# Batch-normalised pair products on one Trainium2 core: the long rows taken in descending instead of ascending order

## The chip, the core and the metric

The kernel runs on one core of one Trainium2 chip. The metric is the device time of one execution in microseconds; the kernel before takes 1881.34 us (median of three runs, 1881.19 to 1881.53). The engines named below are TensorE (PE in the profile), VectorE (DVE), ScalarE (ACT), GpSimd (POOL) and SyncE (SP), which here issues the output transfers. SBUF is the on-chip memory that the engines work in, PSUM the smaller one that TensorE writes to.

## What is computed

Two inputs of 1024 batch rows, 39 fields and 16 elements are multiplied pair by pair, normalised per pair over the batch, and weighted by one 16x16 matrix. There are 741 pairs (r, c) with c < r, and each pair gives a 16x16 block for each batch row: 777 MB of float32 output from about 5 MB of input.

```python
B, F0, F1, E, C = (256, 39, 39, 16, 1)          # the inputs that come have 1024 in place of B
_ROWS, _COLS = np.tril_indices(F1, k=-1)         # 741 pairs
cross = xj[:, rows, :, None] * xi[:, cols, None, :]
mean = jnp.mean(cross, axis=(0, 2, 3), keepdims=True)
var = jnp.mean(jnp.square(cross - mean), axis=(0, 2, 3), keepdims=True)
normed = (cross - mean) * jax.lax.rsqrt(var + BN_EPS)
normed = normed * gamma[None, :, None, None] + beta[None, :, None, None]
out = normed[:, :, None, :, :] * W[None, None, :, :, :]
```

## The kernel before

The kernel first computes a scale s and a shift t for each pair, so that the normalised product is s * (xi * xj) + t. A **row** r holds the pairs (r, 0) to (r, r-1). The 1024 batch rows are 128 partitions by 8 blocks, and a **tile** is one row for two blocks (T = 2): 2 x r slices of 256 elements per partition.

The output buffer `y_sb` is two **slots** of 76 slices. The middle row 19 comes first, as four tiles of half a slot each. Then each long row r shares its slot with the short row 38 - r, so that a slot is always full; row 38 has no partner and fills a slot alone.

```python
half = T * (F - 1)                                # 76
mid = (F - 1) // 2                                # 19
tiles = [(mid, t0, t0 // T * half // 2) for t0 in range(0, NT, T)]
slot = 0
for r in range(mid + 1, F):                       # 20, 21, ... 38
    for t0 in range(0, NT, T):
        tiles.append((r, t0, slot * half))
        if r < F - 1:
            tiles.append((F - 1 - r, t0, slot * half + T * r))
        slot ^= 1
```

Each tile goes through four stages. `scale_xi` (line 167, GpSimd) makes xi * s for the row, into one of two buffers. `products` (lines 145 and 147) makes 16 products for each of the two blocks, each over all pairs of the row; ScalarE takes the first ones and GpSimd the last 4 to 6 of each block. Rows of at most 4 pairs are made on VectorE instead (lines 180 and 190).

```python
split = E - (POOL_I_FIRST[n] if n < 3 else POOL_I_LONG if tiles[n][0] > LONG else POOL_I)
for t in range(T):
    for i in range(E):
        product(n, nc.scalar if i < split else nc.gpsimd, t, i, xs[:, t])
```

`finish` adds the shift and multiplies by the weight. VectorE does that for most pairs, one instruction for each pair (line 284). A share of the pairs goes to GpSimd (lines 270 and 273); in rows over 33, eight pairs, whose shift ScalarE adds (line 268) and which GpSimd weights in two steps of four pairs.

```python
if long:                                          # r > 33
    share = POOL_PAIRS_LONG                       # 8
elif RAW < n < 10:
    share = POOL_PAIRS_FIRST                      # 3
else:
    share = int(r * POOL_SHARE + 0.5) if r > SHORT else 0
p0 = p1 - share                                   # p1 is r // 2 in long rows, else r
... # GpSimd's pairs p0 to p1
for t in range(0, T, size):                       # size is 2, but 1 for tile 1
    for c0, c1 in zip(bounds(n), bounds(n)[1:]):
        for c in [*range(c0, min(c1, p0)), *range(max(c0, p1), c1)]:
            stt(...)                              # line 284, VectorE
        store(n, c0, c1, t, t + size)
```

`bounds` cuts a tile into the pieces in which it is stored: `FIRST_PIECES` for the first tiles, then one piece up to row 24 and two above. In rows over 24 the last piece goes out as two stores, one for each block.

```python
FIRST_PIECES = (
    (0, 1, 3, 6, 10, 14, 19), (0, 4, 9, 14, 19), (0, 4, 11, 19), (0, 9, 19), (0, 10, 20), (0, 9, 18), (0, 10, 20), (0, 9, 18)
)
step = 1 if r > ONE and c1 == r else t_to - t_from        # ONE is 24
for t in range(t_from, t_to, step):
    nc.sync.dma_start(...)                                # line 209
```

The scales and shifts reach all partitions by groups of rows. `spread` copies a group with TensorE into a PSUM bank, and `apply` (lines 493 to 500, three or four small operations on VectorE) folds in gamma and beta. A group is given as (first row, row behind the last, bank, the tile behind which it is applied).

```python
ROW_GROUPS = (
    (19, 20, 0, None), (20, 21, 1, None), (15, 19, 1, 2), (21, 25, 2, 4), (1, 15, 2, 8), (25, 32, 3, 16), (32, 39, 4, 24)
)
SHORT_GROUP = 4
...
for group in range(1, len(ROW_GROUPS)):
    spread(group)
s_short = spread_of[SHORT_GROUP][0][:, 0]
apply(1)
products(1)
scale_xi(2)
for n in range(1, len(tiles)):
    if n + 2 < len(tiles):
        scale_xi(n + 2)
    finish(n)
    for group, (_, _, _, tile_of) in enumerate(ROW_GROUPS):
        if n == tile_of:
            apply(group)
    if n + 1 < len(tiles):
        products(n + 1)
    if n == 32:
        nc.scalar.copy(xj_short, xj_sb[:, :, 1 : SHORT + 1, :])
```

The framework sets the waits: an instruction that writes slices of `y_sb` waits until the transfers that still read them have landed.

Of the kernel before, what the change touches and what calls it, by code (L numbers as in the profile page):

```python
# [16 lines left out]

ONE, LONG = 24, 33
FIRST_PIECES = (
    (0, 1, 3, 6, 10, 14, 19), (0, 4, 9, 14, 19), (0, 4, 11, 19), (0, 9, 19), (0, 10, 20), (0, 9, 18), (0, 10, 20), (0, 9, 18)  # L20
)


# [6 lines left out]


ROW_GROUPS = (
    (19, 20, 0, None), (20, 21, 1, None), (15, 19, 1, 2), (21, 25, 2, 4), (1, 15, 2, 8), (25, 32, 3, 16), (32, 39, 4, 24)
)
SHORT_GROUP = 4


@with_exitstack
def tile_pair_outer_batchnorm(
# [17 lines left out]
    NB, F, E = xi.shape  # L57
# [8 lines left out]
    mid = (F - 1) // 2  # L66
    tiles = [(mid, t0, t0 // T * half // 2) for t0 in range(0, NT, T)]
    slot = 0
    for r in range(mid + 1, F):
        for t0 in range(0, NT, T):  # L70
            tiles.append((r, t0, slot * half))
            if r < F - 1:
                tiles.append((F - 1 - r, t0, slot * half + T * r))
            slot ^= 1

    RAW = 1
# [58 lines left out]
    def view(n):  # L135
        r, _, u = tiles[n]
        return y_sb[:, u : u + T * r, :].rearrange("p (t n) e -> p t n e", t=T)
# [23 lines left out]
    def scale_xi(n):  # L161
        r, t0, _ = tiles[n]
        if r <= SHORT:
            return
        n0 = first[r]
        xs = scaled.tile([P, T, r, E], F32, tag="xs", name=f"xs_{r}_{t0}")
        nc.gpsimd.tensor_tensor(  # L167
            xs,
            xi_sb[:, t0 : t0 + T, 0:r, :],
            s_sb[:, :, n0 : n0 + r, :].to_broadcast([P, T, r, E]),  # L170
            ALU.mult,
        )
        xs_of[n] = xs

    def products(n):

        r, t0, _ = tiles[n]
        if r <= SHORT:
            xs = scaled_short.tile([P, T, r, E], F32, tag="xs_short", name=f"xs_{r}_{t0}")
            nc.vector.tensor_tensor(  # L180
                xs,
                xi_sb[:, t0 : t0 + T, 0:r, :],
                s_short[:, first[r] : first[r] + r]
                .unsqueeze(1)
                .unsqueeze(3)
                .to_broadcast([P, T, r, E]),
                ALU.mult,
            )
            for t in range(T):
                nc.vector.tensor_tensor(  # L190
                    view(n)[:, t].rearrange("p n (i j) -> p n i j", j=E),
                    xs[:, t].unsqueeze(2).to_broadcast([P, r, E, E]),
                    xj_short[:, t0 + t, r - 1 : r, :].unsqueeze(3).to_broadcast([P, r, E, E]),
                    ALU.mult,
                )
            return
        xs = xs_of.pop(n)
# [5 lines that stand above are left out]
    def store(n, c0, c1, t_from=0, t_to=T):  # L203
        r, t0, _ = tiles[n]
        n0 = first[r]

        step = 1 if r > ONE and c1 == r else t_to - t_from
        for t in range(t_from, t_to, step):
            nc.sync.dma_start(  # L209
                out_v[:, t0 + t : t0 + t + step, (n0 + c0) * EE : (n0 + c1) * EE],  # L210
                view(n)[:, t : t + step, c0:c1, :].rearrange("p t n e -> p t (n e)"),
            )
# [27 lines left out]
    def bounds(n):  # L240
        if n < len(FIRST_PIECES):
            return FIRST_PIECES[n]
        r = tiles[n][0]
        pieces = 1 + (r > ONE)
        return tuple(q * r // pieces for q in range(pieces + 1))

    def finish(n):


        r = tiles[n][0]  # L250
        n0 = first[r]
        y = view(n)
        long = r > LONG
        p1 = r // 2 if long else r
        if long:
            share = POOL_PAIRS_LONG
        elif RAW < n < 10:
            share = POOL_PAIRS_FIRST
        else:
            share = int(r * POOL_SHARE + 0.5) if r > SHORT else 0  # L260
        p0 = p1 - share
        step = POOL_PAIRS_LONG // 2 if long else r
        for c0 in range(p0, p1, step):
            c1 = min(c0 + step, p1)
            for c in range(c0, c1):
                t_c = t_sb[:, n0 + c : n0 + c + 1]
                if long:
                    nc.scalar.activation(y[:, :, c, :], y[:, :, c, :], AF.Identity, bias=t_c)  # L268
                else:
                    nc.gpsimd.tensor_scalar(  # L270
                        y[:, :, c, :], y[:, :, c, :], t_c, 1.0, ALU.add, ALU.mult
                    )
            nc.gpsimd.tensor_tensor(  # L273
                y[:, :, c0:c1, :],
                y[:, :, c0:c1, :],
                w_sb.unsqueeze(1).to_broadcast([P, T, c1 - c0, EE]),
                ALU.mult,
            )

        size = 1 if n == RAW else T  # L280
        for t in range(0, T, size):
            for c0, c1 in zip(bounds(n), bounds(n)[1:]):
                for c in [*range(c0, min(c1, p0)), *range(max(c0, p1), c1)]:
                    stt(  # L284
                        y[:, t : t + size, c, :],
                        y[:, t : t + size, c, :],
                        t_sb[:, n0 + c : n0 + c + 1],
                        w_dve.to_broadcast([P, size, EE]),
                        ALU.add,
                        ALU.mult,  # L290
                    )
                store(n, c0, c1, t, t + size)

    with tc.manual_schedule():
# [180 lines left out]
        def spread(group):  # L475
            r0, r1, bank, _ = ROW_GROUPS[group]
            n0, n1 = first[r0], first[r1 - 1] + r1 - 1
            at = used[bank]
            used[bank] = at + 2 * (n1 - n0)
            ps = ps_st[bank][:, at : used[bank]].rearrange("p (x n) -> p x n", x=2)  # L480
            for r in range(r0, r1):
                nc.tensor.matmul(  # L482
                    ps[:, :, first[r] - n0 : first[r] - n0 + r],
                    pick[:, r, :],
                    stq[:, :, 0:r],
                    start=True,
                    stop=True,
                )
            spread_of.append((ps, n0, n1))

        def apply(group):
            ps, n0, n1 = spread_of[group]
            nc.vector.tensor_mul(ps[:, 1], ps[:, 1], st_sb[:, 0, n0:n1])
            if group == SHORT_GROUP:

                nc.vector.tensor_mul(ps[:, 0], ps[:, 0], st_sb[:, 0, n0:n1])
                nc.vector.tensor_copy(st_sb[:, 0, n0:n1], ps[:, 0])
            else:
                nc.vector.tensor_mul(st_sb[:, 0, n0:n1], ps[:, 0], st_sb[:, 0, n0:n1])
            nc.vector.tensor_add(st_sb[:, 1, n0:n1], ps[:, 1], st_sb[:, 1, n0:n1])  # L500
# [8 lines left out]
        for group in range(1, len(ROW_GROUPS)):  # L509
            spread(group)  # L510
        s_short = spread_of[SHORT_GROUP][0][:, 0]
        apply(1)
        products(1)
        scale_xi(2)

# [6 lines that stand above are left out]
                    apply(group)  # L522
            if n + 1 < len(tiles):
                products(n + 1)
            if n == 32:
                nc.scalar.copy(xj_short, xj_sb[:, :, 1 : SHORT + 1, :])


# [26 lines left out]
```

## Time and profile before

| What | Before |
|---|---|
| Device time, median of 3 | 1881.34 us |
| Span of the profiled execution | 1880.0 us |
| VectorE busy | 1720.4 us (92%) |
| ScalarE busy | 1642.7 us (87%) |
| GpSimd busy | 1531.7 us (81%) |
| Output queue, share of the 16 DMA engines | 98.3% |
| Bytes written | 776.99 MB |

Three parts of the profile matter here. A table by stretch gives, for each stretch of time, the busy time of each engine with its number of instructions, then the TensorE clock, the mean share of the 16 DMA engines that was busy, and GB/s; a share well under 1 in a short stretch is time in which the output queue had nothing to move. The timeline lists instructions in order of time, neighbours of one kind merged, with the idle time before them and what ended it. The groups by shape give the busy time and the mean duration of one instruction.

Times in these views are microseconds from the start of the span. A line number such as L284 is that of the kernel before; in the changed kernel the same line has a number one higher.

### The profile page before, as it was taken

How to read it: one execution, taken by the hardware profiler on the slowest of the kernel's cores; microseconds unless marked ns; L12 is line 12 of the kernel's file. 1: busy time of each engine (PE TensorE's matmuls, PEld its weight loads, DVE VectorE, ACT ScalarE, POOL GpSimd, SP SyncE). 2: the span in 40 equal slices, each digit the busy share in tenths (PEclk: the TensorE clock that was granted, in tenths of full speed). 3: DMA queues.
4: the chain of work that ended last, by engine and by line, in shares of the span. 5: the costliest groups of instructions: out<-in, count | busy, mean ns of one | idle time of the engine just before them, and what ended most of it. 6: DMA issues, size and time to landing. Idle time of an engine off the chain costs nothing. (4 is left out here: it accounts for less than half of the span.)

```text
span 1880.0 us, 9660 instructions
## 1 busy us (share of the span) xinstructions
PE 25.5 (1%) x130; PEld 23.0 (1%) x130; DVE 1720.4 (92%) x2625; ACT 1642.7 (87%) x3416; POOL 1531.7 (81%) x1746
## 2 busy tenths in 40 slices
PE   4000000000000000000000000000000000000000
PEld 4000000000000000000000000000000000000000
DVE  8999999998989898989898989898999999988885
ACT  7998989898989798989898989898988888888883
POOL 8999888888888788888888878787888777777873
PEclk8555555555555555555555555555555555555555
DMA  5999999999999999999999999999999999999999
GB/s 197 384 424 426 430 427 428 429 425 426 425 427 424 424 424 424 424 426 425 424 423 425 424 426 424 416 424 424 422 420 425 423 424 422 420 422 415 426 415 411
DMA packets 63994, 783.63 MB, mean 417 GB/s; under 512 B 4784, under 2 KB 6448, under 8 KB 17072
## 3 DMA queue, kind: packets, MB, share of 16 engines
q1 hardware_dynamic: 62624, 779.72, 98.3%
q10 hardware_dynamic: 1296, 3.29, 0.5%
q14 instruction: 73, 0.60, 0.1%
q8 instruction: 1, 0.02, 0.0%
HBM read 6.00 MB, written 776.99 MB: 416 GB/s over the span
## 5 line engine op out<-in xcount | busy, mean ns | idle before, releaser
L284 DVE SCALAR_TENSOR_TENSOR y_sb<-y_sb,st_sb,w_dve 128x512 f32<-128x512 f32 (+1 forms) x2511 | 1651.0, 738 | 132.1 <-issue 119.7
L145 ACT ACTIVATE y_sb<-xs,xj_sb 128x288 f32<-128x288 f32 (+20 forms) x3194 | 1510.7, 567 | 192.9 <-DMA out_dram<-y_sb 163.8
L147 POOL TENSOR_SCALAR y_sb<-xs,xj_sb 128x416 f32<-128x416 f32 (+29 forms) x1126 | 604.7, 560 | 41.2 <-DMA out_dram<-y_sb 28.0
L273 POOL TENSOR_TENSOR y_sb<-y_sb,w_sb 128x2048 f32<-128x2048 f32 (+3 forms) x155 | 517.1, 3342 | 104.0 <-ACT y_sb L268 94.4
L167 POOL TENSOR_TENSOR xs<-xi_sb,st_sb 128x640 f32<-128x640 f32 (+33 forms) x135 | 184.0, 1363 | 171.3 <-ACT y_sb L145 165.1
L270 POOL TENSOR_SCALAR y_sb<-y_sb,st_sb 128x512 f32<-128x512 f32 x291 | 196.8, 691 | 0.1
L268 ACT ACTIVATE y_sb<-y_sb,st_sb 128x512 f32<-128x512 f32 x160 | 100.2, 708 | 1.9
L190 DVE TENSOR_TENSOR y_sb<-xs,ps 128x1024 f32<-128x1024 f32 (+3 forms) x32 | 24.8, 818 | 0.6
L482 PE MATMUL ps<-y_sb 39*128 39x38 f32 (+37 forms) x76 | 16.5, 398 | 2.9 <-DVE y_sb L468 2.9
L482 PEld LDWEIGHTS ps<-y_sb 39*128 39x128 f32 x76 | 16.3, 329 | 3.1 <-DVE y_sb L468 3.1
L346 ACT ACTIVATE y_sb<-y_sb 128x1248 f32<-128x1248 f32 x8 | 9.9, 1243 | 2.8 <-POOL y_sb L335 2.8
L351 DVE TENSOR_REDUCE y_sb<-y_sb 128x78 f32<-128x1248 f32 x8 | 11.2, 1445 | 0.4 <-ACT y_sb L346 0.4
L335 POOL TENSOR_TENSOR y_sb<-xi_sb,y_sb 128x1248 f32<-128x1248 f32 x4 | 9.2, 2320 | 2.8 <-ACT y_sb L384 2.8
L145 ACT ACTIVATE y_sb<-xi_sb,xj_sb 128x304 f32<-128x304 f32 x24 | 11.4, 540 | 0.0
L232 DVE TENSOR_TENSOR y_sb<-y_sb,w_dve 128x2048 f32<-128x2048 f32 (+4 forms) x6 | 10.7, 1839 | 0.1
L325 DVE TENSOR_REDUCE y_sb<-xi_sb 128x39 f32<-128x624 f32 (+1 forms) x6 | 6.1, 1012 | 3.8 <-DMA xi_sb<-in_r_xi_dram 3.8
L335 POOL TENSOR_TENSOR y_sb<-xj_sb,y_sb 128x1248 f32<-128x1248 f32 x4 | 9.2, 2322 | 0.0
L225 POOL TENSOR_SCALAR y_sb<-y_sb,st_sb 128x512 f32<-128x512 f32 x8 | 6.4, 813 | 1.9 <-ACT y_sb L145 1.9
L371 PE MATMUL ps<-y_sb 128*39 128x79 f32 x48 | 7.5, 323 | 16.0 <-DVE y_sb L351 15.9
L325 DVE TENSOR_REDUCE y_sb<-xj_sb 128x39 f32<-128x624 f32 (+1 forms) x6 | 6.1, 1013 | 0.6 <-DMA xj_sb<-in_r_xj_dram 0.6
L223 ACT ACTIVATE y_sb<-y_sb,st_sb 128x512 f32<-128x512 f32 x9 | 6.5, 800 | 0.2 <-ACT y_sb L145 0.2
L371 PEld LDWEIGHTS ps<-y_sb 128*39 128x39 f32 x48 | 5.5, 168 | 18.0 <-DVE y_sb L351 10.7
(59 smaller groups left out, 35.2 us busy)
## 6 DMA issues: line engine op xcount, KB each, us to landing
out_dram<-y_sb SPq DMA_DIRECT2D x25, 2304.0 KB, 14.6
out_dram<-y_sb SPq DMA_DIRECT2D x12, 4352.0 KB, 15.4
out_dram<-y_sb SPq DMA_DIRECT2D x12, 4096.0 KB, 16.3
out_dram<-y_sb SPq DMA_DIRECT2D x10, 4608.0 KB, 14.6
out_dram<-y_sb SPq DMA_DIRECT2D x12, 3840.0 KB, 17.5
out_dram<-y_sb SPq DMA_DIRECT2D x21, 2048.0 KB, 17.0
out_dram<-y_sb SPq DMA_DIRECT2D x12, 3584.0 KB, 18.1
out_dram<-y_sb SPq DMA_DIRECT2D x12, 3328.0 KB, 18.1
```

The lines of the kernel that those rows point to most:

```text
L145: nc.scalar.activation(y, src, AF.Copy, scale=scale)
L147: engine.tensor_scalar(y, src, scale, 1.0, ALU.mult, ALU.mult)
L167: nc.gpsimd.tensor_tensor(xs, xi_sb[:, t0 : t0 + T, 0:r, :], s_sb[:, :, n0 : n0 + r, :].to_broadcast([P, T, r, E]), ALU.mult,)
L190: nc.vector.tensor_tensor(view(n)[:, t].rearrange("p n (i j) -> p n i j", j=E), xs[:, t].unsqueeze(2).to_broadcast([P, r, E, E]), xj_short ...
L268: nc.scalar.activation(y[:, :, c, :], y[:, :, c, :], AF.Identity, bias=t_c)
L270: nc.gpsimd.tensor_scalar(y[:, :, c, :], y[:, :, c, :], t_c, 1.0, ALU.add, ALU.mult)
L273: nc.gpsimd.tensor_tensor(y[:, :, c0:c1, :], y[:, :, c0:c1, :], w_sb.unsqueeze(1).to_broadcast([P, T, c1 - c0, EE]), ALU.mult,)
L284: stt(y[:, t : t + size, c, :], y[:, t : t + size, c, :], t_sb[:, n0 + c : n0 + c + 1], w_dve.to_broadcast([P, size, EE]), ALU.add, ALU.mult,)
L325: nc.vector.tensor_reduce(total[:, t0:t1, part(x)], sources[x][:, t0:t1], AX.X, ALU.add)
L335: nc.gpsimd.tensor_tensor(devs[n % 7], sources[x][:, t0 : t0 + T], shift[:, x : x + 1, :].unsqueeze(3).to_broadcast([P, T, F, E]), ALU.sub ...
L371: nc.tensor.matmul(ps_g[acc][0:F, 0 : 2 * F + 1], lhs, fb[:, t], start=t == 0, stop=t == NT - 1)
L482: nc.tensor.matmul(ps[:, :, first[r] - n0 : first[r] - n0 + r], pick[:, r, :], stq[:, :, 0:r], start=True, stop=True,)
```

## The change

The long rows behind the middle row come in descending order, 38 to 20, each still with its short row. The aim is that the kernel ends with small tiles instead of tiles that fill a slot. Four things go with it:

- The row groups are cut differently, ordered as the rows now come up, and applied later: row 38's group follows tile 1, and no group is applied ahead of tile 1.
- Tiles 4 and 5, now of row 38, are stored in four pieces; the entries for tiles 6 and 7 go.
- The share of three pairs for GpSimd holds for tiles 2 and 3 alone. Tiles 4 to 9, which it covered before, are now long tiles or tiles with a rule of their own.
- The copy of the short rows' xj to PSUM follows tile 5 instead of tile 32, since row 1 comes up at tile 9.

```diff
 FIRST_PIECES = (
-    (0, 1, 3, 6, 10, 14, 19), (0, 4, 9, 14, 19), (0, 4, 11, 19), (0, 9, 19), (0, 10, 20), (0, 9, 18), (0, 10, 20), (0, 9, 18)
+    (0, 1, 3, 6, 10, 14, 19), (0, 4, 9, 14, 19), (0, 4, 11, 19), (0, 9, 19), (0, 10, 19, 29, 38), (0, 10, 19, 29, 38)
 )
@@
 ROW_GROUPS = (
-    (19, 20, 0, None), (20, 21, 1, None), (15, 19, 1, 2), (21, 25, 2, 4), (1, 15, 2, 8), (25, 32, 3, 16), (32, 39, 4, 24)
+    (19, 20, 0, None), (38, 39, 1, 1), (34, 38, 1, 4), (1, 5, 1, 5), (29, 34, 2, 28), (5, 10, 2, 29),
+    (25, 29, 3, 68), (10, 14, 3, 69), (20, 25, 4, 100), (14, 19, 4, 101),
 )
-SHORT_GROUP = 4
+SHORT_GROUP = 3
@@
-    for r in range(mid + 1, F):
+    for r in range(F - 1, mid, -1):
@@
-        elif RAW < n < 10:
+        elif RAW < n < 4:
             share = POOL_PAIRS_FIRST
@@
         s_short = spread_of[SHORT_GROUP][0][:, 0]
-        apply(1)
         products(1)
@@
-            if n == 32:
+            if n == 5:
                 nc.scalar.copy(xj_short, xj_sb[:, :, 1 : SHORT + 1, :])
```

## The prediction, made before the changed kernel was run

> **What bounds the kernel now.** I read four views in this order: the page, tables of busy time by stretch, the timeline around the stretches that stood out, and the groups by shape for durations. From the page, the busy share of the 16 DMA engines by slice, and the bytes:
>
> ```profile
> DMA  5999999999999999999999999999999999999999
> ...
> HBM read 6.00 MB, written 776.99 MB: 416 GB/s over the span
> ```
>
> After the first slice the output queue is busy everywhere. So the time is a startup, plus 777 MB at the queue's own rate, plus the gaps in which the queue has nothing to move. The order of the rows changes no byte; it can only move gaps. I looked for them stretch by stretch (the last two columns are DMA share and GB/s):
>
> ```profile
> 64.00:65.00 1.00, 0.00 (x0) 0.00 (x0) 1.00 (x3) 1.00 (x4) 1.00 (x1) 0.50 0.31 123
> 68.00:69.00 1.00, 0.00 (x0) 0.00 (x0) 1.00 (x3) 1.00 (x4) 1.00 (x3) 0.50 0.00 0
> 78.00:80.00 2.00, 0.00 (x0) 0.00 (x0) 2.00 (x5) 2.00 (x5) 2.00 (x4) 0.50 0.81 340
> 300.00:500.00 200.00, 0.00 (x0) 0.00 (x0) 187.80 (x287) 183.11 (x416) 167.20 (x214) 0.50 1.00 427
> 1215.00:1216.00 1.00, 0.00 (x0) 0.00 (x0) 1.00 (x2) 1.00 (x3) 1.00 (x4) 0.50 0.48 196
> 1830.00:1831.00 1.00, 0.00 (x0) 0.00 (x0) 1.00 (x2) 1.00 (x3) 1.00 (x2) 0.50 0.10 39
> ```
>
> The full rate is 427 GB/s. One pair of a tile (two batch blocks, 262,144 bytes) takes 0.614 us of queue, and a tile of row 38 takes 23.3 us. Adding up the shortfalls of the shares, the queue is short by 2.6 us between 64 and 70, 0.4 us at 78 to 80, 0.8 us at 1215 to 1217 (by the bytes written so far, where row 31 gives way to row 32), 0.5 us at 1662 to 1666 and 1.0 us at 1733 to 1738 (rows 36 and 37), and 1.6 us at 1830 to 1834 (row 38). These sum to about 7 us, and not all of it is in an order's reach. The timeline shows why row 38 starves:
>
> ```profile
> 1819.21 19.84 DVE L284 SCALAR_TENSOR_TENSOR y_sb<-y_sb,st_sb,w_dve 128x512 f32<-128x512 f32 x30 [5.04 <-issue]
> 1819.21 5.01 ACT L268 ACTIVATE y_sb<-y_sb,st_sb 128x512 f32<-128x512 f32 x8
> 1821.92 9.00 POOL L273 TENSOR_TENSOR y_sb<-y_sb,w_sb 128x2048 f32<-128x2048 f32 x2 [8.47 <-ACT y_sb L268]
> 1826.79 15.35 ACT L145 ACTIVATE y_sb<-xs,xj_sb 128x608 f32<-128x608 f32 x22 [2.57 <-DMA out_dram<-y_sb]
> 1830.89 7.49 POOL L147 TENSOR_SCALAR y_sb<-xs,xj_sb 128x608 f32<-128x608 f32 x10
> ```
>
> The columns are start, duration, engine, line, operation, shape and count. A row-38 tile fills a whole slot of the two. Its products may start only when the tile two before has left that slot. Every store of its first piece then waits for products (15.35 us on ScalarE), half the biases (2.7 us), and two weightings on GpSimd (9.0 us), which end at 1830.92; 0.3 us later the queue runs again. That is a chain of 27.1 us + 0.3 us. What covers it is the tile between (23.3 us) plus what the older tile still has queued when the products start. Here the queue went dry at 1830.0, 3.2 us after the next products started at 1826.79; that lead exists because the older tile's last piece goes out as two stores, and the second (19 pairs of one block, 5.8 us) is not waited for by the first half of the products. 27.4 - 23.3 - 3.2 = 0.9 us short, of the order of the 1.6 us seen.
>
> **What the Trainium skill says.** *DMA: Bandwidth & Descriptors*, Specifications, gives a fabric ceiling of 435 GB/s and a limit of about 358 GB/s for one core's HBM. The trace agrees with the first as the wall (427) and not with the second. The same page, Anatomy of one DMA, puts most of a transfer's fixed cost of about 2 us (fitted there on another issuing path) into the write receipt before the semaphore. The trace fits: the half tile ended at 1830.0 - 5.8 = 1824.2, and its waiter started 2.6 us later. *Perfetto Trace Analysis*, Optimization Strategy, says that a gap repeating on the saturated engine can mean too few buffers; the row-38 chain is such a case.
>
> **The change, part by part.** I number tiles as in the list: 0 to 3 are the middle row, tile 4 is the first behind it: row 20 before, row 38 after.
>
> *Groups.* One group of three small VectorE operations (46.92 to 47.63) goes from ahead of tile 1 to behind it, and a later group at 71.48 goes. Tile 1 gains 0.7 us, tile 2 nothing, tile 3 about 0.5 us. The 64 to 70 gaps stay, as tile 2's pieces come no earlier; the 0.4 us at 78 to 80 goes. The queue then runs from 69.2 through the rest of tiles 2 and 3: (7 + 8 + 19) x 0.614 = 20.9 us, dry at 90.1.
>
> *Tile 4 becomes row 38.* Durations come from row 38's own groups in the trace before:
>
> ```profile
> L145 ACT ACTIVATE y_sb<-xs,xj_sb 128x608 f32<-128x608 f32 x88 | 61.4, 789 | 13.3 <-DMA out_dram<-y_sb 8.8 <-DVE y_sb L284 4.4
> L147 POOL TENSOR_SCALAR y_sb<-xs,xj_sb 128x608 f32<-128x608 f32 x40 | 30.0, 779 | 0.0
> L167 POOL TENSOR_TENSOR xs<-xi_sb,st_sb 128x1216 f32<-128x1216 f32 x4 | 9.1, 2273 | 6.8 <-ACT y_sb L145 6.8
> ```
>
> GpSimd sets it. It takes up tile 4's scaling at 60.9, behind the moved group: 2.3 us, then tile 2's share 2.1 + 3.4, tile 3's products 4.0 (72.7), tile 5's scaling 2.3, tile 3's share 5.5 (80.5), and tile 4's ten products at 0.75 us: 88.0. ScalarE is done earlier: 66 middle-row products of 0.44 us from 41.1 end at 70.3, plus 15.4 us, 85.7. VectorE finishes tile 3 at 82 and waits to 88.3. Ten pairs at 0.66 us and 0.9 us from there to the first packet (as at 68.3 to 69.2) give 95.8. **Gap: 95.8 - 90.1 = 5.7 us.** With row 20 it was none: products are half as long and the first piece was issued at 89.8.
>
> *Tile 5* (row 38, slot 1) is covered. Tile 4 lasts in the queue to 95.8 + 23.3 = 119.1. Tile 5's products follow tile 4's biases on ScalarE (93.3 to 108.7), and its first piece is ready near 116.3. The queue runs to 142.4.
>
> *Tile 6* is the second row-38 tile in slot 0. Tiles 4 and 5 are cut into four pieces, so the pair of stores at the end holds 9 pairs instead of 19: the first block ends only 9 x 0.307 = 2.8 us before the tile. With the receipt of 2.6 us, tile 6's products start at 119.1 - 2.8 + 2.6 = 118.9. They end at 134.3; a copy of the short rows' factors now sits there on ScalarE (512 elements, 0.6 us as a product of that size takes); half the biases and the weightings take 11.7 us; tile 6 itself is in two pieces. First packet at 146.9. **Gap: 146.9 - 142.4 = 4.5 us.** Tile 7 starts from tile 5 by the same lag, but the gap has already paid for it: products 142.2, first packet 169.6, against a queue busy to 170.2: none. Tile 8 (row 37) is like the late row-37 tiles, some 0.5 us.
>
> *The late gaps.* Row 38's 1.6 us goes; rows 36 and 37 keep theirs; the 0.8 us at the change of row should go, since a shorter row behind a longer one reaches back less into slots still draining. The end itself is fixed: the queue is full to 1878 before, and after it rows 20 and 18 leave four tiles in the slots, with VectorE at 17 + 16 pairs x 0.66 = 21.8 us against 23.3 us of queue.
>
> *Sum:* + 5.7 + 4.5 + 0.5 - 0.4 - 1.6 - 0.8 = + 7.9 us, some 0.4%. I take off 1 us because order may close small gaps that I did not list: 1881.3 + 6.9 = 1888.2.
>
> **Rivals.** (a) *The queue hides it:* if it carried a longer backlog past tile 3, the waits at tiles 4 and 6 would cost nothing, and the time would be 1881.3 - 0.4 - 1.6 - 0.8 = 1878.5. Against it: the dry stretches at 64 to 80 show that the queue lives from hand to mouth there. (b) *VectorE or ScalarE becomes the bound in the row-38 stage:* 30 pairs x 0.66 = 19.8 us and 15.35 + 5.0 = 20.4 us per tile, both below 23.3, so no; if waits took the slack at every tile of rows 34 to 38, 20 long tiles at 1 us would make 1900. The late stretches lose only 3.1 us in all, which speaks against it. (c) *The tail:* if the old end lost time to its large last tile and the new one did not, the change would win 2 to 3 us more. The queue's 436 GB/s from 1850 to 1870 speaks against it.
>
> **Range and chances.** The two new gaps rest on measured durations and on one lag each, good to about 2 us each; rival (a) in part pulls down to 1882, a repeat of the gap at tiles 8 to 16 pulls up to 1894. Two per cent is 38 us, nearly five times the sum, so "within 2%" is nearly sure.
>
> **What would show it.** In the trace after: VectorE waiting some 6 us before 88; a DMA share near zero from 90 to 96 and again for 4 to 5 us near 143; ScalarE's first tile-6 product near 119, released by an output transfer; no loss at the end. Wrong would be: a full queue from 90 to 150, or a loss spread over hundreds of microseconds.

## The result, and the profile after

The changed kernel takes 1889.32 us (median of six runs, 1889.25 to 1889.52) against 1881.26 us: a ratio of 1.0043, 95% interval 1.0030 to 1.0056. It is 8.1 us slower. The prediction said 1888.2 us.

| What | Before | After |
|---|---|---|
| Span of the profiled execution | 1880.0 us | 1887.5 us |
| VectorE / ScalarE / GpSimd busy | 1720 / 1643 / 1532 us | 1725 / 1643 / 1526 us |
| Output queue, share of 16 DMA engines | 98.3% | 97.9% |
| Time behind 60 us with no packet under way on any DMA engine | 2.6 us | 9.8 us |
| Last store: latest DMA engine behind the first | 0.2 us | 5.9 us |

The last two rows are counted from the DMA packets and the landing events of the trace. Each store lands as 16 events, one for each DMA engine.

The work is the same, so the difference is in the gaps. First, the page of the kernel after:

```profile
DMA  5899999999999999999999999999999999999998
...
HBM read 6.00 MB, written 776.99 MB: 415 GB/s over the span
```

The digit lost is the second one, and the last slice is down to 8. The table by stretch of the kernel after opens these up (last two columns: DMA share and GB/s; a packet counts in the stretch in which it starts):

```profile
78.00:80.00 2.00, 0.00 (x0) 0.00 (x0) 2.00 (x4) 2.00 (x4) 2.00 (x2) 1.00 0.52 217
91.00:92.00 1.00, 0.00 (x0) 0.00 (x0) 1.00 (x2) 1.00 (x3) 1.00 (x1) 1.00 0.03 8
93.00:94.00 1.00, 0.00 (x0) 0.00 (x0) 1.00 (x2) 1.00 (x3) 1.00 (x1) 1.00 0.00 0
95.00:96.00 1.00, 0.00 (x0) 0.00 (x0) 1.00 (x2) 1.00 (x3) 1.00 (x1) 1.00 1.00 420
143.00:144.00 1.00, 0.00 (x0) 0.00 (x0) 1.00 (x2) 1.00 (x2) 1.00 (x1) 1.00 0.00 0
1878.00:1880.00 2.00, 0.00 (x0) 0.00 (x0) 0.00 (x0) 0.00 (x0) 0.00 (x0) 1.00 1.03 442
1880.00:1882.00 2.00, 0.00 (x0) 0.00 (x0) 0.00 (x0) 0.00 (x0) 0.00 (x0) 1.00 0.26 111
1882.00:1884.00 2.00, 0.00 (x0) 0.00 (x0) 0.00 (x0) 0.00 (x0) 0.00 (x0) 1.00 0.15 65
1884.00:1886.00 2.00, 0.00 (x0) 0.00 (x0) 0.00 (x0) 0.00 (x0) 0.00 (x0) 1.00 0.06 28
```

There are two new wholly dry stretches, at 91.6 to 95.2 us (tile 4) and 143.0 to 145.9 us (tile 6). The end differs in kind: from 1880 us on the queue works at a quarter of its rate and less. A share of 0.26 is 4 engines of 16, and 0.06 is one. Before the change the stream ran at full rate until it stopped at 1878 us:

```profile
1876.00:1878.00 2.00, 0.00 (x0) 0.00 (x0) 0.00 (x0) 0.00 (x0) 0.00 (x0) 0.50 1.09 467
1878.00:1880.00 2.00, 0.00 (x0) 0.00 (x0) 0.00 (x0) 0.00 (x0) 0.00 (x0) 0.50 0.00 0
```

The timeline of the kernel after shows what released tiles 4 and 6:

```profile
72.10 10.62 DVE L285 SCALAR_TENSOR_TENSOR y_sb<-y_sb,st_sb,w_dve 128x512 f32<-128x512 f32 x16 [1.31 <-POOL y_sb L148]
79.93 7.49 POOL L148 TENSOR_SCALAR y_sb<-xs,xj_sb 128x608 f32<-128x608 f32 x10
87.45 19.84 DVE L285 SCALAR_TENSOR_TENSOR y_sb<-y_sb,st_sb,w_dve 128x512 f32<-128x512 f32 x30 [4.73 <-POOL y_sb L148]
117.56 15.34 ACT L146 ACTIVATE y_sb<-xs,xj_sb 128x608 f32<-128x608 f32 x22 [4.76 <-DMA out_dram<-y_sb]
132.81 0.57 ACT L526 COPY ps<-xj_sb 128x512 f32<-128x512 f32 x1
135.95 9.01 POOL L274 TENSOR_TENSOR y_sb<-y_sb,w_sb 128x2048 f32<-128x2048 f32 x2 [0.71 <-ACT y_sb L269]
```

VectorE waits for GpSimd's products of tile 4 until 87.45. Tile 6's products wait for an output transfer until 117.56, and its weightings end at 144.96; the store behind them is issued at 144.98, and the first packet comes at 145.88.

### The profile page after: what moved, and what is told of

Read it like the earlier page. It is cut to its first block, busy times and chain, and to the rows that moved or that the text cites. A ratio compares the mean times of both kernels' runs of the same rounds, so it can differ in the third digit from the quotient of the medians.

```text
span 1887.5 us, 9618 instructions
## 1 busy us (share of the span) xinstructions
PE 26.0 (1%) x130; PEld 23.3 (1%) x130; DVE 1724.7 (91%) x2637; ACT 1642.7 (87%) x3416; POOL 1526.1 (81%) x1743
## 3 DMA queue, kind: packets, MB, share of 16 engines
q1 hardware_dynamic: 62624, 779.72, 97.9%
## 5 line engine op out<-in xcount | busy, mean ns | idle before, releaser
L146 ACT ACTIVATE y_sb<-xs,xj_sb 128x512 f32<-128x512 f32 (+21 forms) x3194 | 1510.7, 566 | 194.8 <-DMA out_dram<-y_sb 162.9
L148 POOL TENSOR_SCALAR y_sb<-xs,xj_sb 128x464 f32<-128x464 f32 (+27 forms) x1126 | 604.3, 560 | 1.4 <-DMA out_dram<-y_sb 1.4
L168 POOL TENSOR_TENSOR xs<-xi_sb,st_sb 128x1216 f32<-128x1216 f32 (+33 forms) x135 | 184.0, 1363 | 218.9 <-ACT y_sb L146 207.2
L191 DVE TENSOR_TENSOR y_sb<-xs,ps 128x256 f32<-128x256 f32 (+3 forms) x32 | 24.8, 817 | 0.6
L146 ACT ACTIVATE y_sb<-xi_sb,xj_sb 128x304 f32<-128x304 f32 x24 | 11.4, 536 | 0.0
## 6 DMA issues: line engine op xcount, KB each, us to landing
out_dram<-y_sb SPq DMA_DIRECT2D x23, 2304.0 KB, 17.8
out_dram<-y_sb SPq DMA_DIRECT2D x12, 3840.0 KB, 17.8
```

The lines of the kernel that those rows point to most:

```text
L146: nc.scalar.activation(y, src, AF.Copy, scale=scale)
L148: engine.tensor_scalar(y, src, scale, 1.0, ALU.mult, ALU.mult)
L168: nc.gpsimd.tensor_tensor(xs, xi_sb[:, t0 : t0 + T, 0:r, :], s_sb[:, :, n0 : n0 + r, :].to_broadcast([P, T, r, E]), ALU.mult,)
L191: nc.vector.tensor_tensor(view(n)[:, t].rearrange("p n (i j) -> p n i j", j=E), xs[:, t].unsqueeze(2).to_broadcast([P, r, E, E]), xj_short ...
```

## The experiments

Two theories stood against each other. **A, the slowest DMA engine:** what counts is the time in which no DMA engine moves anything; partly dry stretches are engines waiting for the latest one, since a store has landed only when all 16 have. **B, the tail:** the late end is a loss of its own. The table collects the runs. Ratios are to the kernel before, with 95% intervals; "dry" is the time behind 60 us with no packet on any DMA engine; "late" is the last store's latest engine behind its first. The kernel before, run beside each of them, took 1881.3 to 1881.4 us.

| Run | us | Ratio | Dry, us | Late, us |
|---|---|---|---|---|
| before | 1881.3 | | 2.6 | 0.2 |
| after | 1889.3 | 1.0043 (1.0030 to 1.0056) | 9.8 | 5.9 |
| row 20 first (e1) | 1881.7 | 1.0002 (0.9993 to 1.0011) | 2.3 | 5.1 |
| two pieces (e2) | 1890.6 | 1.0049 (1.0034 to 1.0064) | 11.8 | 5.9 |
| more fetches (e3) | 1898.2 | 1.0087 (1.0071 to 1.0104) | 6.2 | 6.3 |
| scaling later (e4) | 1887.6 | 1.0033 (1.0021 to 1.0045) | 7.6 | 5.8 |
| e1, store on fewer engines (f1) | 1893.1 | 1.0063 (1.0046 to 1.0080) | 2.3 | 18.3 |
| e1, finer pieces (f2) | 1881.9 | 1.0003 (0.9994 to 1.0011) | 0.7 | 5.2 |
| f1 and f2 (f3) | 1893.1 | 1.0062 (1.0047 to 1.0077) | 0.8 | 18.4 |
| before, more fetches (f4) | 1890.7 | 1.0050 (1.0035 to 1.0065) | 0.9 | 0.2 |
| e1, fewer instructions (g1) | 1880.1 | 0.9993 (0.9984 to 1.0001) | 2.3 | 4.4 |
| e1, shorter instructions (g2) | 1882.0 | 1.0005 (0.9996 to 1.0013) | 2.3 | 5.2 |

### e1: row 20 first, then descending

```diff
-    for r in range(F - 1, mid, -1):
+    for r in (mid + 1, *range(F - 1, mid + 1, -1)):
```

Groups, first pieces and GpSimd's share follow the new order (for row 20 those of the kernel before).

> Row 20 first, as before the change, then 38 down to 21; the end is that of the changed kernel (21 and 17 instead of 20 and 18). Theory A (slowest DMA engine): what the change costs is the time in which no DMA engine at all moves anything, 9.8 us behind 60 us in the changed kernel against 2.6 us before, and the 6 us by which four of the 16 engines come late at the end cost nothing that was not paid before in short dry stretches of the other twelve. With row 20 first a backlog has built up by the time row 38 comes, so the stretches at 91 and 142 us go: 1889.3 - 7.2 = 1882 us or a little under, although the last store still lands with four engines some 6 us late. Theory B (the tail): the late landing at the end is a loss of its own, about 5 us, which small tiles and a full queue bring; the start is then only part of it and the time stays near 1886.

Measured: 1881.74 us. The stretches at 91 and 143 us are gone. The table by stretch of this run shows the end:

```profile
1870.00:1872.00 2.00, 0.00 (x0) 0.00 (x0) 0.00 (x0) 0.00 (x0) 0.00 (x0) 1.00 1.10 470
1872.00:1874.00 2.00, 0.00 (x0) 0.00 (x0) 0.00 (x0) 0.00 (x0) 0.00 (x0) 1.00 0.55 235
1874.00:1876.00 2.00, 0.00 (x0) 0.00 (x0) 0.00 (x0) 0.00 (x0) 0.00 (x0) 1.00 0.20 87
1876.00:1878.00 2.00, 0.00 (x0) 0.00 (x0) 0.00 (x0) 0.00 (x0) 0.00 (x0) 1.00 0.08 35
```

The ragged end of 5 us is there, and yet the time is that of the kernel before, which has none. Theory B falls: the loss of the change is at its start, and row 38 meeting a queue without a backlog is the cause. The backlog can be read from the stores. In the kernel after, all earlier stores had landed by 91.8 us when tile 4's first was issued at 94.3. In e1 row 38's first store was issued at 183.7, and the one ahead of it landed at 185.5. The ragged end costs about what the late rows' partly dry stretches cost before; the sums are in the part on the prediction.

### e2 and e4: the two gaps, one at a time

```diff
-    (0, 1, 3, 6, 10, 14, 19), (0, 4, 9, 14, 19), (0, 4, 11, 19), (0, 9, 19), (0, 10, 19, 29, 38), (0, 10, 19, 29, 38)
+    (0, 1, 3, 6, 10, 14, 19), (0, 4, 9, 14, 19), (0, 4, 11, 19), (0, 9, 19)
```

> The changed kernel, with tiles 4 and 5 in two pieces instead of four. Theory A: the first piece of tile 4 now waits for both weightings on GpSimd, 87.4 + 2.7 + 9.0 + 0.3 = 99.4 us, so the first dry stretch grows from about 4 to about 8 us; tile 6's products start earlier against the end of tile 4, and the second stretch shrinks from 3 to about 1.4 us. Sum about + 2.7 us: 1892 us. Rival: the extra pair of pieces was harmless to tile 6 and the second stretch stays at 3 us: 1893.5 us.

Measured: 1890.64 us, 1.3 us above the kernel after (their runs don't overlap). The first stretch is 8.5 us with no packet at all. The second, now at 147 us, has 0.1 us of it left, and its share lacks 0.5 us:

```profile
98.00:99.00 1.00, 0.00 (x0) 0.00 (x0) 1.00 (x3) 1.00 (x3) 1.00 (x1) 1.00 0.00 0
99.00:100.00 1.00, 0.00 (x0) 0.00 (x0) 1.00 (x2) 1.00 (x2) 1.00 (x2) 1.00 0.00 0
146.00:148.00 2.00, 0.00 (x0) 0.00 (x0) 2.00 (x4) 2.00 (x4) 2.00 (x3) 1.00 0.76 321
```

So the four pieces of tile 4 buy 4.9 us of dry time at tile 4 and cost 2.8 us at tile 6; that they cost something there is what the prediction worked out. Both stretches moved the way of theory A, but its sum of + 2.7 us was too large: the dry time rose by 2.0 us and the time by 1.3.

```diff
-            if n + 2 < len(tiles):
+            if n + 2 < len(tiles) and n != 3:
                 scale_xi(n + 2)
@@
                 products(n + 1)
+            if n == 3:
+                scale_xi(5)
```

> The changed kernel with tile 5's scaling (2.3 us on GpSimd) moved from ahead of tile 4's products to behind them. Theory A: GpSimd, which ends tile 4's products at 87.4 us and releases VectorE, ends at 85.2, beside ScalarE at 84.9; the first dry stretch shrinks by 2.2 us and the time falls to 1887.1 us. Rival: ScalarE or the queue sets the start of tile 4 and nothing changes, 1889.3.

Measured: 1887.58 us, 1.7 us below the kernel after. The timeline of this run:

```profile
77.89 7.50 POOL L148 TENSOR_SCALAR y_sb<-xs,xj_sb 128x608 f32<-128x608 f32 x10
85.42 15.23 DVE L285 SCALAR_TENSOR_TENSOR y_sb<-y_sb,st_sb,w_dve 128x512 f32<-128x512 f32 x23 [2.50 <-POOL y_sb L148]
```

GpSimd ends 2.0 us earlier, VectorE starts 2.0 us earlier, and the dry time falls by 2.1 us. GpSimd's queue of work ahead of tile 4 does set the first gap.

### e3 and f4: more instructions to fetch

In the kernel after, 12 engines land each store within 0.3 us, and the other four come later and later: by 0.4, 0.6, 1.2 and 1.5 us near 500 us, and by 3.3, 3.6, 5.5 and 6.2 us near 1440. Then a stretch comes in which for 1.9 us exactly four engines work, and the other twelve do not:

```profile
1458.00:1460.00 2.00, 0.00 (x0) 0.00 (x0) 2.00 (x4) 2.00 (x5) 1.92 (x3) 1.00 0.51 215
1460.00:1462.00 2.00, 0.00 (x0) 0.00 (x0) 2.00 (x5) 2.00 (x5) 2.00 (x2) 1.00 0.60 255
```

The trace has one other stream that lasts through the run: single packets of 8 KB on the instruction queue, 0.31 us each.

```diff
+            for _ in range(10):
+                nc.tensor.matmul(ps_s[:, 0:8], w_sb[:, 0, 0:128], w_sb[:, 0, 0:8], start=True, stop=True)
```

> The changed kernel plus ten small matmuls behind each tile on the otherwise idle TensorE, into a PSUM bank that is free by then; nothing waits for them and the output is untouched. They only have to be fetched: 1500 matmuls. Theory A says that the four late DMA engines are late because they also fetch the engines' instructions (packets of 8 KB on the instruction queue, 0.31 us each; before the one long dry stretch at 1460 us the four lags sum to 18.5 us). If fetches are what makes an engine late, a new engine becomes the latest, or the latest gets later: some 46 more packets, 14 us, so the time rises by about 6 us if TensorE's fetches have a DMA engine of their own (the latest has 6 to 8 us now) and by up to 14 us if they share one. If the lag has another cause (memory, the partitions an engine serves), the time stays at 1889.3.

Measured: 1898.16 us, 8.8 us above the kernel after. The part of the page on DMA queues, first of the kernel after, then of this run:

```profile
q14 instruction: 73, 0.60, 0.1%
q8 instruction: 1, 0.02, 0.0%
```

```profile
q8 instruction: 24, 0.39, 0.1%
q14 instruction: 73, 0.60, 0.1%
```

The matmuls brought 23 packets of 16 KB, all before 670 us, which took 21.4 us (22.6 with the one there was). Nothing waits for these matmuls, and the output's bytes are the same. Its packets took no longer either: the median is 0.615 us per 16 KB between 100 and 600 us, with and without the matmuls, so it is not TensorE's work that slows them. Near 500 us one DMA engine is 4.4 us late instead of 1.5. If the latest engine works through all but the dry time, the rise of 8.8 us with 3.6 us less dry time means 12.4 us more work for it; where the rest of the 21.4 us went was not separated. That the rise lies in the expected range is partly luck: the range came from 14 us of packets, and with 21.4 us the same working gives 13 us or more.

> The kernel before with the same ten matmuls behind each tile as in e3, whose fetches (24 packets of 16 KB, 22.6 us) made the changed kernel 8.8 us slower, while the time in which no engine moved anything fell by 3.6 us: 12.4 us more work for the latest engine. Theory A (the latest DMA engine sets the time in both orders, and the short dry stretches of the others in the late rows only wait for it): the kernel before has 2.6 us of such time to give, so it gets slower by 10 to 12 us: 1891.5 to 1893.5 us, with long rows waiting longer. Rival: in the ascending order the late rows have slack for a late engine, so that part of the lag is absorbed: under 1888 us.

Measured: 1890.66 us, 9.4 us above the kernel before. That is above the rival's limit and just under the range of theory A. The dry time fell by 1.7 us, so that by the same sum the latest engine has 11.1 us more work. It sets the time in the ascending order too, but some of the lag may have been absorbed.

### g1 and g2: fewer instructions, or the same number made short

```diff
             for i in range(E):
+                if r < mid and 0 < i < split:
+                    continue
                 product(n, nc.scalar if i < split else nc.gpsimd, t, i, xs[:, t])
@@
                 for c in [*range(c0, min(c1, p0)), *range(max(c0, p1), c1)]:
+                    if SHORT < r < mid and c % 2:
+                        continue
```

> Row 20 first, as in e1, with instructions left out in the short rows 5 to 18 (its output lacks them): ScalarE makes one product per block instead of all of its share, 1232 instructions fewer of 3416, and VectorE finishes every other pair, some 280 fewer of 2637. All output is still stored. Theory A: fetching instructions is what makes four DMA engines late (5.1, 3.7, 3.0 and 1.9 us at the end of e1, in the order of how many instructions the engines have), and the latest sets the time. ScalarE then has fewer than VectorE, whose 3.7 us shrink to about 3.3: the end comes some 1.8 us earlier, 1880 us, and the last store's latest landing is about 3.3 us behind the first. Rival: the lateness has another source, and as the queue bounds the kernel, less work on the engines changes nothing: 1881.7.

The control keeps the number of instructions and shortens them:

```diff
+        if r < mid and i and engine is nc.scalar:
+            y, src = y[:, 0:1], src[:, 0:1]
@@
+                    wide = 1 if SHORT < r < mid and c % 2 else size
                     stt(
-                        y[:, t : t + size, c, :],
-                        y[:, t : t + size, c, :],
+                        y[:, t : t + wide, c, :],
+                        y[:, t : t + wide, c, :],
```

> The control to g1: row 20 first, as in e1, with as many instructions as e1, but the same ones made short instead of left out (ScalarE's products over one pair instead of all, VectorE's over one block instead of two; the output lacks the rest). Theory A: the same fetches, so the same lateness of 5 us at the end and the same time, 1881.7 us. Rival (the lighter load on ScalarE and VectorE is what helps): as g1.

Measured: 1880.05 us (1879.68 to 1880.42) for g1 and 1882.04 us (1881.69 to 1883.12) for g2, on the same chip; their runs don't overlap. The instruction queue of g1 has 12 packets fewer (that of g2 has the 73 of the others):

```profile
q14 instruction: 61, 0.50, 0.1%
```

Fewer instructions (1232 on ScalarE, 265 on VectorE) help by 2.0 us against the same number made short, and by 1.7 us against e1; a lighter load alone does not. One of the four lags falls from 1.9 to 0.7 us, but the latest is 4.4 us and not the 3.3 expected, so which lag belongs to which engine's instructions stays open.

### f1, f2, f3: two attempts to do better

f1 cuts the last tile (17 pairs) into pieces of 8 and 9 pairs, and splits the store of the first, 128 partitions, into two:

```diff
+        if n == len(tiles) - 1 and c0 == 0:
+            for a, b in ((0, 108), (108, P)):
+                nc.sync.dma_start(...)            # partitions a to b
+            return
```

> Row 20 first, as in e1, and one store of the last tile (pairs 0 to 7, 2.1 MB) issued as two transfers of 108 and 20 partitions instead of one of 128, so that they should run on 12 and 10 of the 16 DMA engines (the Trainium skill, DMA: Bandwidth & Descriptors, on why a DMA increments its semaphore by 16: the largest number up to 16 that divides the partitions, and the lowest-numbered engines). Theory A: the end waits for the latest of four late engines (5.1 us in e1). If the late ones are among the four left out, they are relieved of 4.9 us and the others get up to 1.8 us more: 1881.7 - 3.3 = 1878.4 us. If the late ones are among the twelve, they get later still, by up to 1.8 us: 1883.5 us. If the lateness is no matter of load on an engine, nothing changes beyond the smaller pieces, 1881.7.

Measured: 1893.08 us, a miss in the bad direction and far larger than either estimate. In the last store four engines now land first (0 to 0.5 us), and of the other twelve all but one come 6 to 9 us or more behind, the latest 18.3 us. So the load did move off four engines, as the Trainium skill's rule has it (*DMA: Bandwidth & Descriptors*, Why a DMA increments its semaphore by 16 and not by 1), and they were not the late ones. Why the latest got some 6 us more than the split accounts for was not settled.

```diff
-(0, 4, 11, 19), (0, 9, 19), (0, 10, 20), (0, 9, 18),
+(0, 4, 8, 12, 16, 19), (0, 4, 9, 14, 19), (0, 5, 10, 15, 20), (0, 4, 9, 14, 18),
```

> Row 20 first, as in e1, with tiles 2 to 5 stored in five, four, four and four pieces instead of three, two, two and two. Theory A: the dry time left in e1 behind 60 us is 2.2 us, where the queue waits for pieces of tiles 2 and 3 to be finished; a smaller piece arrives earlier by 0.66 us for each pair that it lacks, so most of that goes: 1881.7 - 1.8 = 1880 us. Rival: the queue only runs dry at other points, since VectorE makes pairs hardly faster than the queue takes them: 1881.7.

Measured: 1881.87 us, no gain, although the dry time fell from 2.3 to 0.7 us. Tables by stretch, first of e1, then of f2:

```profile
40.00:100.00 60.00, 9.37 (x45) 9.23 (x44) 59.61 (x105) 60.00 (x137) 57.95 (x76) 1.00 0.96 390
120.00:140.00 20.00, 0.00 (x0) 0.00 (x0) 19.93 (x35) 20.00 (x46) 19.67 (x27) 1.00 0.99 413
```

```profile
40.00:100.00 60.00, 9.64 (x46) 9.50 (x45) 59.59 (x105) 60.00 (x137) 57.95 (x75) 1.00 1.00 398
120.00:140.00 20.00, 0.00 (x0) 0.00 (x0) 19.93 (x34) 20.00 (x47) 19.67 (x27) 1.00 0.97 403
```

To 100 us f2 has moved 8 GB/s more over 60 us, 0.5 MB; by 300 us that lead is gone (108.3 MB in e1 and 108.2 in f2 since 40 us). The first lines show what it was paid with. f2 moves 398 GB/s at a share of 1.00, and e1 390 at 0.96, which is 406 at a full share: a smaller piece means smaller packets (64,800 on the output queue instead of 62,624), and those move less in the same time. Over the run the output's packets take 1.9 us more on each engine (a mean of the 16), against 1.5 us of dry time saved. The time is the rival's, but its reason is not the only one: VectorE is full in both runs too, and how much that adds was not separated.

> Row 20 first with both changes of f1 and f2. Theory A: they touch different ends of the kernel and add up: 1876.5 us if the late engines are among the four left out, 1881.7 if they are not.

Measured: 1893.05 us, as f1. No version beat the kernel before by more than the runs scatter: e1 equals it. g1 leaves out part of the output and is no candidate.

## Why the prediction was right, and where it was not

The time, 1889.3 us, lies in the range of 1882 to 1894 and within 1.1 us of the 1888.2 predicted; the change is 8.1 us against 6.9. The causes named, row 38's long chains met by an empty queue at tiles 4 and 6, are the ones that e1, e2 and e4 show. That the sum came so close is partly luck. The table, counted from the packets, gives the time in which a DMA engine had none under way, as a mean of the 16:

| Idle time of a DMA engine, us | Before | After | Row 20 first (e1) |
|---|---|---|---|
| 60 to 150 us | 3.4 | 11.4 | 3.1 |
| 150 to 1860 us | 6.1 | 1.6 | 2.5 |
| From 1860 us to the last packet | 0.1 | 4.8 | 4.2 |
| Sum | 9.6 | 17.8 | 9.8 |

The output is the same, so the sums differ about as the times do. The start cost 8.0 us, where the prediction's terms give + 9.8 (5.7 + 4.5 - 0.4). The long middle gave back 4.4 us, where it had - 2.9 (0.5 - 1.6 - 0.8 - 1.0). The end cost 4.7 us, where it had nothing. The errors of - 1.8, - 1.5 and + 4.7 nearly cancel: 8.2 us in all against 6.9. Point by point:

- **Tile 4 (predicted + 5.7 us).** The shares at 90 to 95 us lack 4.2 us. GpSimd's products end at 87.4 as worked out (88.0), and the first packet comes at 95.2 (95.8). The queue ran dry later, near 91.0 on most engines and not at 90.1, because it had already stopped once before.
- **The gap at 78 to 80 us (predicted to go, - 0.4).** It grew to 1.2 us. The step overlooked that tile 4's scaling for row 38, 2.3 us instead of 1.3, also delays tile 3's products on GpSimd, on which VectorE waits: it starts tile 3 at 72.10 after a wait of 1.31 us, and not 0.5 us earlier than before. Against the 0.4 us of before that is + 0.8; with tile 4 the two terms are + 5.0 us measured against + 5.3.
- **Tile 6 (+ 4.5).** Between 142 and 148 us the shares lack 3.4 us, 2.9 of it wholly dry. Tile 6's products started at 117.56 instead of 118.9. The copy took 0.57 us, as assumed.
- **Two delays that the prediction misread.** It put the 2.6 us between a store's end and the start of its waiter down to the write receipt, and said that the trace fits. The landing events show something else. Before, the store that the products at 1826.79 waited for had landed on 12 engines by 1824.95 and on the latest at 1826.69, so 1.7 us of the 2.6 are the latest engine's lag. At tile 6 the two are 116.48 and 117.45, and the products started at 117.56. It also let the queue run again 0.3 us behind the weightings of row 38 (1830.92). The store was issued at 1830.95 and the packets came at 1831.85: 0.9 us, as at every wholly dry stretch of the kernel after. Its chain is 28.0 us, not 27.4.
- **Tile 7** covered, as predicted; **tile 8** (+ 0.5): no dry stretch was left.
- **The late gaps (- 1.6 and - 0.8) and the hedge (- 1.0).** They did go, and with smaller ones not listed they gave back 4.4 us, but nothing was won by it. At 1830 us the share was 0.10, not 0: two engines still worked for 0.6 us, then one until 1831.9. A shortfall of the share is in part engines that wait for the latest one. e1 has none of row 38's late stretches, a ragged end instead, and nearly the same time.
- **"The end itself is fixed", "no loss at the end".** This is the step that failed. The end is ragged for 6 us, 4.8 us as a mean of the engines against 0.1 before. The late gaps and the ragged end are in large part the same lag of the latest engine, paid at two places. Counted by the latest engine alone, the dry time rose by 9.8 - 2.6 = 7.2 us and the time by 8.1; the last 0.9 us stays unassigned.
- **Rivals.** (a), that the queue hides the waits, falls by the dry stretches: the backlog at tile 4 was nil. With a backlog it is right, which is e1. (b), a loss in every long row, falls: between 150 and 1400 us the engines of the kernel after were idle for less than 0.01 us. (c), a win at the tail, falls by the ragged end.

## What to carry to other kernels

When transfers bound a kernel, look for stretches in which no DMA engine works; a share of 0.1 or 0.5 can be engines that wait for a later one, and removing it may only move that wait to the end. Put tiles with a long chain of work behind a stage that has built a backlog, not first: the same tiles cost 8 us at the start and about 1 us of partly dry time eight tiles later. A finer first piece helps its own tile and can delay the one that reuses its buffer.

## What the runs showed of the hardware

In the kernel after, four of the 16 DMA engines fall behind, by up to 6.2 us near 1440 us and by 2.3 to 5.9 us at the end, while the others stay within 0.3 us of each other. Adding instructions (23 packets more on one queue, 21.4 us) cost 8.8 and 9.4 us in the two orders; leaving out some 1500 saved 1.7 us, and shortening the same ones saved nothing. The Trainium skill, *Runtime: NRT & Kernel Launch*, Instruction fetch mechanics, says that instructions are refilled in blocks of 16 KiB over a DMA queue and that the cost is mostly hidden. The trace shows 16 KB packets for TensorE and 8 KB packets on the other queue. In this kernel, bound by its transfers, the refill is not hidden: it takes time from the output.
